# Moving a shared expert behind its 16 routed experts, and loading 8 experts' weights piece by piece among the next stage's rows, in a four-layer kernel

## The chip, the cores and the metric

The kernel runs on one core of a Trainium2 chip. The core has five engines with instruction queues of their own, each worked off in order: TensorE (PE, matrix products), VectorE (DVE), ScalarE (ACT), GpSimd (POOL) and SyncE (SP, which here issues most DMA transfers). The metric is the device time of one execution in microseconds (us), the median over several runs; the profile is one further execution.

## The reference

Four layers follow one another, each an "attention" (a token mixer) and an ffn, each behind a residual sum and a layer norm. x is (4, 1024, 128) in float32: 4096 tokens of 128 values.

```python
x = _layernorm(x + _L0_attn_ref(x, ...))   # cumulative sums over tokens
x = _layernorm(x + _L0_ffn_ref(x, ...))    # quantized linear layer
x = _layernorm(x + _L1_attn_ref(x, ...))   # complex diagonal recurrence
x = _layernorm(x + _L1_ffn_ref(x, ...))    # 16 experts, top 4, + shared expert
x = _layernorm(x + _L2_attn_ref(x, ...))   # causal softmax attention, 16 heads
x = _layernorm(x + _L2_ffn_ref(x, ...))    # 8 experts, top 2
x = _layernorm(x + _L3_attn_ref(x, ...))   # Toeplitz mixing, gated
x = _layernorm(x + _L3_ffn_ref(x, ...))    # experts, top 4, + shared expert
```

The change touches the ffn of layer 1 and the weights of the ffn of layer 2:

```python
# _L1_ffn_ref, E = 16 experts, F = 128
topk_idx, tw = _route(x, router_w, bias)             # 4 experts of each token
h = einsum('td,edf->etf', x, gate_w); u = einsum('td,edf->etf', x, up_w)
y = einsum('etf,efd->etd', silu(h) * u, down_w)
routed = einsum('etd,te->td', y, combine)
sh = silu(x @ sh_gate_w) * (x @ sh_up_w) @ sh_down_w # every token, 256 wide
return routed + sh

# _L2_ffn_ref, E = 8 experts, common weights plus low-rank parts of each expert
act = silu(x @ w_gate.T + d1[e]) * (x @ w_up.T + d3[e])
```

## The kernel before, in words

**Tokens.** x and its transpose stay in SBUF as 32 tiles of 128 tokens, in four quarters of 8 tiles. The first half ("a") is quarters 0 and 1, the second ("r") quarters 2 and 3. The halves run staggered: while one is in layer 1, the other is still in layer 0.

**Experts.** A routed ffn takes four steps. The router gives each token its experts and a place in each expert's list (`l1_route`, `positions`). `spread` (L1317) writes every token's row into the lists in DRAM (`l1ra`, `l1rr`): one indirect DMA (L1305) by POOL for each tile and choice, so 64 for a half with 4 experts a token. `small_experts` runs through the lists: 18 groups of 4 tiles, whose rows SP loads as `xg` (L1336); PE transposes them (`tp`), multiplies by gate and up (`gu`) and down; SP stores the result `yg` to `l1ya` or `l1yr` (L1762). A further part for longer lists stands in a branch. `collect` (L1385) fetches each token's results back by indirect DMA of POOL (`yt`, 5 buffers of four) and adds them to x with their weights (DVE, L1396).

**Shared expert.** `l1_shared` loads swg, swu and swd and runs four blocks of 4 tiles: two products `pg` and `pu` a half block (L157), hidden `hs` (DVE), the down product `py`, and the addition to x (DVE, L830). `l1_close` collects, norms a quarter, saves it (`xsave`, L840) and transposes it anew.

**Weights of layer 2.** `l2_weights` loads 1.5 MB (`in_l2_big`, in the profile `ld<-in_l_big`) and works out each expert's full weights on PE and ACT, since common weights and low-rank parts can be summed beforehand; 24 pieces go to DRAM (`wall_30`, L1450). `l2_wall` (L1467) loads them back into SBUF as `wall`, 8 transfers of 768 KB on SP (L1472), and `l2_experts` uses them.

**Order.** The stages are Python generators that emit instructions and yield planned microseconds. `chain` runs generators one after the other, `abreast` runs one beside another, `mix(main, side, pace, drain)` emits `side` whenever the planned time of `main` has run ahead, `when` yields until a condition holds. `queued` (L231) keeps what is emitted as side behind the latest main instruction of PE, ACT, DVE and POOL; SP's queue has no such tie. A list scheduler then settles each engine's order by dependencies and priority. Which step may begin is also set by memory: a pool's space is reused when its last reader has finished.

**Stages around the change** (`all`, L1882). First half: scatter to `l1ra`; then `l1_shared(a)` and `l1_experts(a)` as main, with `l0_ffn` and `l1_attn` of quarters 2 and 3 as side; then `l2_weights` and the rest of that side as main, with `l1_close(a)` as side. Second half: `l2_attn(0)` beside routing and scatter of r; then the 8 loads of `l2_wall`; then `l1_experts(r)` and `l1_shared(r)` as main, with `routed(a2)` (routing and scatter of the first half's rows for layer 2, list `l2ra`) as side; then `l2_experts(a2)` beside `l1_close(r)`.

Of the kernel before, what the change touches and what calls it, by code (L numbers as in the profile page):

```python
# [41 lines left out]
E2, F2, R2, K2 = 8, 512, 16, 2  # L42
# [32 lines left out]
class Kernel:  # L75
# [737 lines left out]
    def l1_shared(self, part):  # L813

        nc, x = self.nc, self.x
        with ExitStack() as ctx:
            cp = self.pool(ctx, "l1sc" + part.name)
            hp = self.pool(ctx, "l1sh" + part.name, 2)
            ps = self.pool(ctx, "l1sp" + part.name, 2, space=PSUM)
            swg = self.load(cp, self.ins["l1_swg"])  # L820
            swu = self.load(cp, self.ins["l1_swu"])
            swd = self.load(cp, self.ins["l1_swd"])
            for blk in range(part.t0 // 4, (part.t0 + part.nt) // 4):
                h = self.tile(hp, [P, 2, BLK], "hs")
                for c in range(2):
                    f = slice(c * P, (c + 1) * P)
                    self.glu(ps, hp, h[:, c, :], swg[:, f], swu[:, f], blk)
                py = self.down(ps, h, swd, 2)
                tl = slice(blk * 4, blk * 4 + 4)
                nc.vector.tensor_tensor(x[:, tl, :], py, x[:, tl, :], ALU.add)  # L830
                yield (5.5,)

    def l1_close(self, part, yp):

        nc, x = self.nc, self.x
        for q in range(part.q0, part.q0 + part.nq):
            yield from self.collect("l1", part, K1, yp, (q - part.q0) * QT, QT)
            self.norm(self.quarter(q))
            tl = slice(q * QT, (q + 1) * QT)
            nc.sync.dma_start(out=self.xsave[:, tl, :], in_=x[:, tl, :])  # L840
            yield (6.0,)
            for g in range(2):
                self.turned(self.side, q * QT + g * 4, tag="s")
                yield (1.5,)
# [619 lines left out]
            yield from self.positions(cp, "l2" + part.name, mask, w, part.nt, E2, K2)  # L1464
            yield (6.0,)

    def l2_wall(self, ctx):  # L1467
        cp = self.pool(ctx, "l2fw")
        wall = self.tile(cp, [P, E2 * 3 * F2], "wall")
        for e in range(E2):  # L1470
            c = slice(e * 3 * F2, (e + 1) * 3 * F2)
            self.nc.sync.dma_start(out=wall[:, c], in_=self.wall2[:, c])  # L1472
        return wall

    def l2_experts(self, part, wall):
# [406 lines left out]
    def all(self):  # L1882
        a, rest = self.first, self.rest
        b, c = rest
        r = self.both[1]
        a2, m2, n2 = self.by_rows
        with ExitStack() as ctx:
            lgp = self.pool(ctx, "l2lg")
            self.l2_lg = self.tile(lgp, [P, NT, E2], "lg")
            with ExitStack() as early:  # L1890

                self.l0_setup(early)
                self.l2_wr = self.load(lgp, self.ins["l2_wr"])
                self.run(self.l0_attn((0, 1)))
                self.l1_setup()
                self.l2_setup()
                self.zero_lists("l1")
                self.run(self.l0_ffn((0, 1)))
                self.run(self.l1_attn((0, 1)))

                self.run(self.l1_route(a))
                self.run(self.mix(self.l0_attn((2, 3), True), self.spread("l1", a, K1)))
                self.zero_lists("l2", "l3")
                with ExitStack() as c2:
                    wall = self.l1_wall(c2)
                    yp = self.pool(c2, "l1ya", 5, right=True)
                    side = self.chain(self.l0_ffn((2, 3), True), self.l1_attn((2, 3), True))
                    self.run(self.mix(self.chain(self.l1_shared(a), self.l1_experts(a, wall)), side, 2.0, False))
                    self.run(self.mix(self.abreast(self.l2_weights(), side), self.l1_close(a, yp)))
            with ExitStack() as c2:  # L1910
                wall = self.l1_wall(c2)
                self.run(self.mix(self.l2_attn(0), self.chain(self.l1_route(r), self.spread("l1", r, K1))))
                wall2 = self.l2_wall(c2)
                yp = self.pool(c2, "l1yr", 5, right=True)
                self.run(self.mix(self.chain(self.l1_experts(r, wall), self.l1_shared(r)), self.routed(a2)))
                self.run(self.mix(self.l2_experts(a2, wall2), self.l1_close(r, yp)))
            listed = lambda name: lambda: name in self.listed
            on = self.served(
                self.chain(self.rows_in(a2), self.onward(a, True)),
                (lambda: self.rows_done >= B + 2, self.routed(m2)),  # L1920
                (lambda: self.rows_done == 2 * B, self.routed(n2)),
            )
            self.run(self.mix(self.l2_attn(1), on, drain=False))
            with ExitStack() as c3:
                with ExitStack() as c2:
                    wall = self.l2_wall(c2)
                    self.press(on, listed("l2m"))
                    self.run(self.mix(self.l2_experts(m2, wall), on, drain=False))
                    self.press(on, lambda: {"l2n", "routed l3a"} <= self.listed)
                    sw, wall3 = self.l3_wall(c3, True)  # L1930
                    on = self.chain(on, self.rows_in(m2))
                    self.run(self.mix(self.l2_experts(n2, wall), on, drain=False))
                self.press(on, listed("l3a"))
                yp = self.pool(c3, "l3y", 8)

                on = self.chain(
                    on, self.collect("l2", n2, K2, yp, which=(0, 1, 4, 5)),
                    self.abreast(
                        self.chain(self.l3_attn(b), self.mark("mixed l3b"), self.l3_route(b)),
                        self.collect("l2", n2, K2, yp, which=(2, 3, 6, 7)),  # L1940
                    ),
                    self.abreast(
                        self.chain(self.spread("l3", b, K3), self.when(listed("made l3a")), self.last(a, yp)),
                        self.chain(self.l3_attn(c), self.mark("mixed l3c"), self.l3_route(c)),
                    ),
                    self.spread("l3", c, K3), self.when(listed("made l3b")), self.last(b, yp),
                )
                self.run(self.mix(self.chain(self.l3_shared(a, sw), self.l3_experts(a, wall3)), on, 0.75, False))
                hold = self.pool(c3, "l3hold", 2)
                for p in (b, c):  # L1950
                    self.press(on, listed("mixed l3" + p.name))
                    sh = self.tile(hold, [P, QT, D], "sh")
                    self.run(self.mix(self.l3_shared(p, sw, sh), on, 0.75, False))
                    self.press(on, listed("l3" + p.name))
                    self.run(self.mix(self.l3_experts(p, wall3), on, 0.75, p is c))
                    s = slice(p.t0, p.t0 + QT)
                    self.nc.vector.tensor_tensor(self.x[:, s, :], sh, self.x[:, s, :], ALU.add)
                self.run(self.close(c, yp))
        bad = self.nc.values_load(self.flag[0:1, 0:1], min_val=0, max_val=1)
        with self.tc.If(bad > 0):  # L1960
            with ExitStack() as ctx:
                lgp = self.pool(ctx, "l2lg2")
                self.l2_lg = self.tile(lgp, [P, NT, E2], "lg")
                self.l2_wr = self.load(lgp, self.ins["l2_wr"])
                self.l2_attn_general()
                for p in self.by_rows:
                    self.run(self.routed(p))
                    with ExitStack() as c2:
                        self.run(self.l2_experts(p, self.l2_wall(c2)))
                    self.run(self.rows_in(p))  # L1970
                for p in self.parts:
                    self.run(self.onward(p))
                    with ExitStack() as c2:
                        sw, wall = self.l3_wall(c2)
                        self.run(self.l3_shared(p, sw), self.l3_experts(p, wall))
                        self.run(self.last(p, self.pool(c2, "l3y" + p.name, 5)))
# [165 lines left out]
```

## Time and profile before

| what | value |
|---|---|
| times of 3 runs | 2420.16, 2432.44, 2435.95 us |
| median | 2432.44 us |
| the profiled execution: its time / its span | 2430.2 / 2428.4 us |
| mean granted PE clock of it | 0.821 |
| busy share of the span: PE, DVE, ACT, POOL | 66%, 52%, 33%, 32% |
| bytes moved by DMA | 187.11 MB, mean 77 GB/s |

How to read the profile: times are microseconds from the start of the span, unless marked ns. A timeline row gives the start, the busy time of a group of like instructions, the engine, the line in the kernel, the operation, output<-inputs by the kernel's names, the count, and in brackets how long the engine had been idle before and what ended that. "SPq" and the like are the engine's instruction queue, in which DMA is issued. "PEld" is the loading of weights into PE. A row of windows gives start and end of a stretch, its length, the busy time of each engine in it with the number of instructions, the granted PE clock (1.00 is full), the mean busy share of the 16 DMA engines, and what they moved. "<-issue" stands for idle time in which the engine waited for nothing that the profile shows.

### The profile page before, as it was taken

Reading aid. Unit: us, or ns where it says so; the run is one execution under the profiler, and the core shown is the slowest. Engines: PE = TensorE matmul, PEld = TensorE weight load, DVE = VectorE, ACT = ScalarE, POOL = GpSimd, SP = SyncE. Lnnn points to the kernel's source line nnn. Section 1 sums busy time; section 2 is a strip of 40 time slices with the busy share of each in tenths; the row PEclk is TensorE's granted clock in tenths of the full one; section 3 lists DMA queues with packets and bytes.
Section 4 is the critical chain, followed back from the end, with each engine's and each line's share of the span. In section 5 each row is a group of like instructions: output and inputs, shape, how many; then the busy total and the mean of one; then the engine's idle time right before and its main releaser. Section 6 shows DMA issues by size and latency. Waiting matters only on the chain. (4 is left out here: it accounts for less than half of the span.)

```text
span 2428.4 us, 27065 instructions
## 1 busy us (share of the span) xinstructions
PE 1597.9 (66%) x9017; PEld 952.6 (39%) x9017; DVE 1272.6 (52%) x3628; ACT 804.3 (33%) x1161; POOL 780.6 (32%) x701
## 2 busy tenths in 40 slices
PE   6535776866671675677969787887726798357160
PEld 2214433743330344544623232344414486145160
DVE  8767895655670564324535674573602265236233
ACT  5511372322330332212336554632201164223030
POOL 5531285145227002234132002002272200735724
PEclk9766788988785888888979998988867899679575
DMA  9930002334201014312130000031411131222232
GB/s 308 288 107 0 14 34 81 118 113 151 77 29 52 16 64 149 97 46 74 41 104 21 1 1 18 1 118 35 160 66 35 39 112 50 76 76 65 89 88 68
DMA packets 215531, 187.11 MB, mean 77 GB/s; under 512 B 16528, under 2 KB 194064, under 8 KB 214864
## 3 DMA queue, kind: packets, MB, share of 16 engines
q1 hardware_dynamic: 194672, 142.29, 18.5%
q0 software_dynamic: 20704, 42.86, 5.7%
q8 instruction: 84, 1.38, 0.2%
q14 instruction: 71, 0.58, 0.1%
HBM read 88.49 MB, written 96.60 MB: 76 GB/s over the span
## 5 line engine op out<-in xcount | busy, mean ns | idle before, releaser
L1059 ACT ACTIVATE pr<-sc 128x1024 f32<-128x1024 f32 x288 | 279.7, 1021 | 318.3 <-PE sc L157 189.2
L157 PE MATMUL gu<-ld,xgT 128*128 x640 | 173.4, 416 | 77.2 <-issue 39.2
L157 PE MATMUL sc<-qm,kT 32*128 32x512 f32 (+3 forms) x1536 | 200.3, 558 | 16.9 <-issue 9.7
L157 PE MATMUL s<-pr,va 128*32 128x512 f32 (+3 forms) x1536 | 173.9, 521 | 46.1 <-issue 26.3
L157 PEld LDWEIGHTS gu<-ld,xgT 128*128 128x128 f32 x640 | 125.5, 207 | 105.9 <-issue 50.0
L169 DVE COPY hT<-tp 128x512 f32<-128x512 f32 x118 | 81.0, 686 | 151.0 <-remote 75.8
L157 PE MATMUL gu<-wall,xgT 128*128 x304 | 156.2, 640 | 2.7 <-ACT xgT L167 2.0
L165 PE MATMUL tp<-ld,xg 128*128 128x128 f32 x396 | 67.2, 299 | 130.1 <-DMA xg<-l3rc 48.5
L165 PE MATMUL tp<-ld,hg 128*128 128x128 f32 x624 | 100.5, 282 | 77.0 <-issue 39.7
L1065 DVE TENSOR_TENSOR pr<-pr,ld 128x512 f32<-128x512 f32 (+1 forms) x160 | 92.3, 581 | 102.6 <-ACT pr L1059 96.5
L1744 DVE TENSOR_TENSOR hg<-sg,gu 128x256 f32<-128x256 f32 x160 | 65.7, 417 | 152.0 <-ACT sg L1743 104.2
L167 ACT COPY xgT<-tp 128x512 f32<-128x512 f32 x99 | 57.9, 586 | 243.5 <-PE tp L165 84.5
L157 PEld LDWEIGHTS sc<-qm,kT 32*128 32x128 f32 x1536 | 85.3, 196 | 117.2 <-issue 78.2
L165 PEld LDWEIGHTS tp<-ld,hg 128*128 128x128 f32 x624 | 79.3, 145 | 129.3 <-issue 74.1
L1743 ACT ACTIVATE sg<-gu 128x256 f32<-128x256 f32 x160 | 60.9, 385 | 166.4 <-PE gu L157 71.9
L1305 POOL DMA_INDIRECT l1ra<-x,posl1a x64 | 94.9, 1482 | 60.7 <-DVE posl1a L1280 41.5
L1502 ACT ACTIVATE sg<-gu 128x512 f32<-128x512 f32 x76 | 45.2, 597 | 206.5 <-PE gu L157 115.1
L1305 POOL DMA_INDIRECT yt<-l1yr,posl1r x64 | 60.7, 948 | 139.6 <-DVE x L1396 79.3
L165 PEld LDWEIGHTS tp<-ld,xg 128*128 128x128 f32 x396 | 50.3, 153 | 135.7 <-issue 83.7
L157 PEld LDWEIGHTS s<-pr,va 128*32 128x32 f32 x1536 | 38.6, 112 | 155.4 <-issue 108.0
L1305 POOL DMA_INDIRECT l1rr<-x,posl1r x64 | 62.5, 976 | 96.3 <-DVE posl1r L1280 77.1
L1305 POOL DMA_INDIRECT yt<-l1ya,posl1a x64 | 70.0, 1094 | 69.9 <-DVE x L1396 29.3
(444 smaller groups left out, 3505.8 us busy)
## 6 DMA issues: line engine op xcount, KB each, us to landing
wall<-wall SPq DMA_DIRECT2D x16, 768.0 KB
l3ra<-zero SPq DMA_DIRECT2D x1, 6144.0 KB
ld<-in_l_w SPq DMA_DIRECT2D x2, 3072.0 KB
wall<-we SPq DMA_DIRECT2D x24, 256.0 KB
ld<-in_l_w SPq DMA_DIRECT2D x1, 6144.0 KB
l1ra<-zero SPq DMA_DIRECT2D x1, 5120.0 KB
l1rr<-zero SPq DMA_DIRECT2D x1, 5120.0 KB
xg<-l3ra SPq DMA_DIRECT2D x20, 256.0 KB
```

The costliest lines, as they stand in the source:

```text
L157: return self.nc.tensor.matmul(out, lhsT, rhs, start=start, stop=stop)
L165: nc.tensor.transpose(pt[:, k * P : (k + 1) * P], s, self.ident)
L167: nc.scalar.copy(dst, pt[:, : n * P])
L169: nc.vector.tensor_copy(dst, pt[:, : n * P])
L1059: nc.scalar.activation(pr, sc[h], AF.Exp)
L1065: nc.vector.tensor_tensor(d, d, cst["tril"].unsqueeze(1).unsqueeze(1).to_broadcast([P, 2, n, P]), ALU.mult)
L1305: ins = self.nc.gpsimd.indirect_dma_start(**kw)
L1502: nc.scalar.activation(sg, gu[:, 0, :], AF.Silu)
L1743: nc.scalar.activation(sg, pg[:, :, 0, :], AF.Silu)
L1744: nc.vector.tensor_tensor(h[:, 2 * c : 2 * c + 2, :], sg, pg[:, :, 1, :], ALU.mult)
```

## The change

It has two parts. In the first half the shared expert of layer 1 goes from ahead of the 16 experts to behind them: it is then emitted in front of `l2_weights` and the rest of the side, and `l1_close(a)` runs beside all three. `l1_shared` notes when it is fully emitted, and `l1_close` holds each quarter's norm until then. In the second half `l2_wall` returns its 8 loads as a generator that yields 2.0 planned us after each, and they head the side of `l1_experts(r)`, with `routed(a2)` behind them, where before all 8 were emitted ahead of that stage. No instruction is added or removed by either part; the transfers and operations are the same in another order.

```diff
--- before.py
+++ after.py
@@ -829,12 +829,14 @@
                 tl = slice(blk * 4, blk * 4 + 4)
                 nc.vector.tensor_tensor(x[:, tl, :], py, x[:, tl, :], ALU.add)
                 yield (5.5,)
+        self.listed.add("shared l1" + part.name)
 
     def l1_close(self, part, yp):
 
         nc, x = self.nc, self.x
         for q in range(part.q0, part.q0 + part.nq):
             yield from self.collect("l1", part, K1, yp, (q - part.q0) * QT, QT)
+            yield from self.when(lambda: "shared l1" + part.name in self.listed)
             self.norm(self.quarter(q))
             tl = slice(q * QT, (q + 1) * QT)
             nc.sync.dma_start(out=self.xsave[:, tl, :], in_=x[:, tl, :])
@@ -1464,12 +1466,21 @@
             yield from self.positions(cp, "l2" + part.name, mask, w, part.nt, E2, K2)
             yield (6.0,)
 
-    def l2_wall(self, ctx):
+    def l2_wall(self, ctx, later=False):
+
         cp = self.pool(ctx, "l2fw")
         wall = self.tile(cp, [P, E2 * 3 * F2], "wall")
-        for e in range(E2):
-            c = slice(e * 3 * F2, (e + 1) * 3 * F2)
-            self.nc.sync.dma_start(out=wall[:, c], in_=self.wall2[:, c])
+
+        def load():
+            for e in range(E2):
+                c = slice(e * 3 * F2, (e + 1) * 3 * F2)
+                self.nc.sync.dma_start(out=wall[:, c], in_=self.wall2[:, c])
+                yield (2.0,)
+
+        if later:
+            return wall, load()
+        for _ in load():
+            pass
         return wall
 
     def l2_experts(self, part, wall):
@@ -1905,14 +1916,15 @@
                     wall = self.l1_wall(c2)
                     yp = self.pool(c2, "l1ya", 5, right=True)
                     side = self.chain(self.l0_ffn((2, 3), True), self.l1_attn((2, 3), True))
-                    self.run(self.mix(self.chain(self.l1_shared(a), self.l1_experts(a, wall)), side, 2.0, False))
-                    self.run(self.mix(self.abreast(self.l2_weights(), side), self.l1_close(a, yp)))
+                    self.run(self.mix(self.l1_experts(a, wall), side, 2.0, False))
+                    on = self.chain(self.l1_shared(a), self.abreast(self.l2_weights(), side))
+                    self.run(self.mix(on, self.l1_close(a, yp)))
             with ExitStack() as c2:
                 wall = self.l1_wall(c2)
                 self.run(self.mix(self.l2_attn(0), self.chain(self.l1_route(r), self.spread("l1", r, K1))))
-                wall2 = self.l2_wall(c2)
+                wall2, loads = self.l2_wall(c2, True)
                 yp = self.pool(c2, "l1yr", 5, right=True)
-                self.run(self.mix(self.chain(self.l1_experts(r, wall), self.l1_shared(r)), self.routed(a2)))
+                self.run(self.mix(self.chain(self.l1_experts(r, wall), self.l1_shared(r)), self.chain(loads, self.routed(a2))))
                 self.run(self.mix(self.l2_experts(a2, wall2), self.l1_close(r, yp)))
             listed = lambda name: lambda: name in self.listed
             on = self.served(
```

In the order that the scheduler gives, SP issues xg, xg, xg, two pieces, xg, two pieces, xg, a piece, a store of y, a piece, a store, xg, a piece, a store, a piece, and then xg and stores alone. In the first half SP issues swg, swu and swd, in_l_big and the weight stores behind the last y store of the experts; DVE has the last part of quarter 3's quantize, then the four shared blocks, then the first additions of `collect`.

## The prediction

> **What bounds the kernel now.** I read the busy totals first, then the timeline around the two places that the change touches, then windows by stage.
>
> No engine bounds the whole: TensorE (PE) is busiest, at 66%.
>
> ```profile
> PE 1597.9 (66%) x9017; PEld 952.6 (39%) x9017; DVE 1272.6 (52%) x3628; ACT 804.3 (33%) x1161; POOL 780.6 (32%) x701
> ```
>
> So I price each stage by itself. First place: the layer-1 ffn of the first half, from the last scatter to the last xsave (us from the span's start).
>
> ```profile
> 395.29 0.96 POOL L1305 DMA_INDIRECT l1ra<-x,posl1a  x1 [0.31 <-issue]
> 399.70 2.07 PE L157 MATMUL pg<-xT,ld 128*128 128x512 f32 x2 [11.87 <-DMA ld<-in_l_swg]
> 432.49 1.04 PE L165 MATMUL tp<-ld,xg 128*128 128x128 f32 x8
> 513.70 1.02 POOL L1305 DMA_INDIRECT yt<-l1ya,posl1a  x1 [21.98 <-DMA l1ya<-yg]
> 518.92 2.04 PE L157 MATMUL s<-ld,ld 128*128 128x512 f32 x2 [9.25 <-DMA ld<-in_l_big]
> 557.06 2.19 DVE L1396 SCALAR_TENSOR_TENSOR x<-yt,wkl1a,x 128x128 f32<-128x128 f32 x8
> 559.25 0.94 POOL L1305 DMA_INDIRECT yt<-l1ya,posl1a  x1 [17.10 <-DVE x L1396]
> 638.97 0.32 SPq L840 DMA_DIRECT2D xsave<-x  x1
> ```
>
> The shared expert holds PE from 399.70 to the experts at 432.49 (32.8 us); 81.2 us later the first row is gathered. From there POOL and the attention of quarters 2 and 3 share the time: 20 gathers fill the buffers, and the rest wait until DVE comes to its adds at 557.06.
>
> ```profile
> core 0: us, PE busy (x) PEld busy (x) DVE busy (x) ACT busy (x) POOL busy (x), PEclk, DMA share, GB/s
> 557.00:641.00 84.00, 41.38 (x152) 22.23 (x151) 47.02 (x182) 18.75 (x37) 47.36 (x44) 0.76 0.43 141
> 1033.00:1058.00 25.00, 13.61 (x36) 6.38 (x36) 3.31 (x5) 2.39 (x4) 18.98 (x20) 0.70 0.24 62
> 1058.00:1073.00 15.00, 14.01 (x64) 9.91 (x64) 4.90 (x8) 2.39 (x4) 0.00 (x0) 0.87 0.08 22
> 732.00:772.00 40.00, 8.61 (x20) 2.39 (x20) 2.05 (x6) 0.00 (x0) 30.38 (x32) 0.50 0.13 52
> ```
>
> In 557 to 641 no engine is full. The three rows below it say why: while POOL issues indirect DMAs the others thin out. In 1033 to 1058 shared blocks of the second half run beside 20 gathers, and PE works 13.61 of 25 us; right after, without gathers, 14.01 of 15. In 732 to 772, beside 32 scatters, PE is down to 8.61 of 40.
>
> Second place: layer-1 experts of the second half, with 8 loads of 768 KB (L1472) in front.
>
> ```profile
> 900.00:922.00 22.00, 4.54 (x22) 3.83 (x23) 6.85 (x31) 0.00 (x0) 0.00 (x0) 0.61 0.86 322
> ```
>
> ```profile
> 901.69 4.17 SPq L1472 DMA_DIRECT2D wall<-wall  x8
> 906.22 27.45 SPq L1336 DMA_DIRECT2D xg<-l1rr  x7
> 921.65 1.97 PE L165 MATMUL tp<-ld,xg 128*128 128x128 f32 x8 [10.66 <-DMA xg<-l1rr]
> 950.55 0.96 POOL L1305 DMA_INDIRECT l2ra<-x,posl2a  x1 [160.17 <-DVE posl2a L1280]
> 987.42 3.39 PE L157 MATMUL gu<-ld,xgT 128*128 x8 [28.06 <-issue]
> 1033.12 0.98 POOL L1305 DMA_INDIRECT yt<-l1yr,posl1r  x1 [42.13 <-DMA l1yr<-yg]
> 1033.68 2.04 PE L157 MATMUL pg<-xT,ld 128*128 128x512 f32 x2 [4.30 <-DMA ld<-in_l_swg]
> 1069.68 3.84 SPq L1336 DMA_DIRECT2D xg<-l2ra  x3
> 1072.36 0.69 DVE L830 TENSOR_TENSOR x<-py,x 128x512 f32<-128x512 f32 x1 [1.92 <-PE py L157]
> ```
>
> The DMA engines are 0.86 busy at 322 GB/s and PE waits 10.66 us for the first rows, which queue behind 6 MB. PE stalls again (28.06 us) in the burst of scatters from 950.55.
>
> **Part 1, the shared expert behind the experts.** Step by step:
>
> Experts start. The last scatter ends at 396.25. A store needs some 2.5 us to be seen by a reader (the last expert store is issued about 511, its reader goes at 513.70) and an xg load 2.8 us to PE (1069.68 to PE at 1072.50). So PE starts at 396.25 + 2.5 + 2.8 ≈ 401.5, and not at 432.49: 31 us earlier. The 3 MB of weights are in: at 399.70 swg, queued behind them on SP, had landed.
>
> Experts. 81.2 us, and some 5 more: in the schedule both quantizes of quarters 2 and 3 lie beside them, where one lay beside the shared expert, and with a quantize PE was busy 15.76 of 20 us (470 to 490), without 19.53 (450 to 470). Bounds 0 and 10. First gather: 401.5 + 86 ≈ 487.5, 26 earlier.
>
> Shared expert. SP issues swg, swu and swd behind the last y stores, as for the second half, where PE then ran beside 20 gathers from 1033.68 to 1073.05: 39 us. DVE has leftovers of the quantize in its queue ahead of the first shared block: 4 more. Bounds: 22 (four blocks at the 5.5 us of the undisturbed two) and 45. So 487.5 + 43 = 530.5. Queued behind it are in_l_big, whose memory comes free with it, and on DVE the first adds, which POOL's later gathers need: these start about 531 instead of 557.
>
> Weights of layer 2 and attention. From the issue of in_l_big (512.03) to PE's use of it (518.92) is 7 us: 537.5. Then come a rest of the ffn of quarter 3 (14), and attention: quarter 2 took 31.5 (525.66 to 557.14, the thin stretch of 531 to 539 costing about half its length), quarter 3 took 49.1 (561.62 to 610.7, with about 22 lost): 28 each unstarved, 56. The 24 stores of the layer-2 weights move on SP behind this; their readers, the loads of 901, have time to spare. The 3 MB load of the second half's layer-1 weights falls behind 23 of these stores and is due only at 921.
>
> Starvation. The 44 later gathers (44 × 1.26 = 55 us by the scatters' pace) run beside this attention. Before they cost it about 22 us (of 25 in 579 to 586 and 588 to 606, where DVE did one small operation per 2 us). I take 15, because more of them fall beside matmul work than beside small DVE operations; bounds 5 and 35.
>
> Tail. Norm of quarter 1 needs the last gathers: 24 adds at 0.29, the last gather and the norm, 17. End: 537.5 + 14 + 56 + 15 + 17 = 639.5 against 638.97: +0.5, between −27 and +20 with the bounds. What the 31 us gave is spent on a shared expert that is dearer beside gathers (43 + 7 for a load that it now holds back, against 33).
>
> The wait put into l1_close adds no semaphore by itself: norm reads the x that the shared adds write. It holds quarter 0's norm on DVE and behind it the first xsave; 12 weight stores queue on SP behind that xsave, none urgent.
>
> A rule of the Trainium skill speaks for more: "SBUF — State Buffer", section "Who interferes with whom", has PE and ACT never wait for another engine's SBUF access, and DVE contend with GpSimd only in certain modes. By it four shared blocks beside gathers would cost 22 us, not 39, and the whole about 2410 us. The rows of 1033 and of 732 disagree: there PE issues one matmul per 1.4 us, as below. The measurement decides; these sentences enter no sum.
>
> ```profile
> 752.22 0.37 PE L157 MATMUL s<-pr,va 128*32 128x128 f32 x1 [2.00 <-issue]
> ```
>
> **Part 2, eight loads behind the first groups.** On SP three xg loads now go first, then the pieces, among xg and y stores. Removed: 8 issues in front (4.17 us) and the queue in the DMA engines. PE's first work moves from 921.65 to about 912.5, held by DVE's copy in l2_attn's last step, which ends at 909.06, and a landing of 2.8: −9. Given back: the sixth to ninth xg now stand on SP behind y stores (which wait for their group) and pieces, where before they had 9 to 10 us of lead. A piece takes 768 KB / 322 GB/s = 2.4 us of all DMA engines; two or three in front of an xg that is due cost some 5. Bounds 0 and 12. Routing is emitted 16 planned us later, so the burst starts about 956; its 38 us stall stays inside the experts' stage (18 groups × 3.6 = 65 us of work), so moving it is worth 0. If it slid past the last y stores it would delay the gathers by some 6. Sum: −4, bounds −9 and +3. l2's experts need the pieces only at 1072.
>
> **Sum.** 2430.2 + 0.5 − 4 ≈ 2427. The profiled execution (span 2428.4, 1.8 outside it) is 2 us under the median of 2432.44, so I leave it.
>
> **Rivals.** (a) The shared expert is not starved. For it: before, it ran in 32.8 us beside a quantize, and its last two blocks of the second half took 5.5 each. Against: the row of 1033. Then part 1 gives its −27: 2430.2 − 27 − 4 ≈ 2399. (b) Slower: the later gathers, freed early, form one long burst beside the attention and stop it, as in 732 to 772 where PE kept 22%. Of 55 us, 43 or more are then lost (78%), 28 over my 15, and with the shared expert at its upper 45 and a second wait of POOL for adds behind quarter 3's work (17.10 before) some 40 in all: 2427 + 40 ≈ 2467. It decides from about 39 of the 55 us lost. Against: before, the same 44 gathers cost 22, because buffers fill and POOL waits for DVE, five at a time. (c) The pieces give back all of part 2, each xg being late by one piece: 4 to 9 us more, 2431 to 2436.
>
> **How the numbers follow.** 1% is 24 us, about what a measurement of this kernel can tell from no change. Forecast 0.48, (a) 0.2, (b) 0.2, (c) 0.12. Forecast and (c) lie within 1%, save some 0.02 at the slow end of their bounds and 0.01 at the fast end; of (a), 0.18 passes −24; of (b), all. That makes faster 0.19, within 0.59, slower 0.22. The range goes from (a)'s 2399 to 2459, where the lower part of (b) is in; the forecast's own bounds are 2430.2 − 36 and 2430.2 + 23.
>
> **What would show it.** First tp<-ld,xg of the first half near 401 (late if the rows land late); first l1ya gather near 487; shared pg to its last L830 add 39 to 45 us (22: rival a); first s<-ld,ld near 537; last xsave near 640 (over 665: rival b). In the second half PE's first tp near 912, the first l1yr gather near 1029. Wrong altogether if a later stage, untouched by the diff, changes its length by more than a few us.

## The result, and the profile after

The changed kernel takes 2433.09 us (median of 12 runs, 2427.39 to 2442.53), the kernel before 2430.57 us in 12 runs beside it: a ratio of 1.0025, 95% interval 1.0005 to 1.0046. Measured again later beside another set of runs it was 1.0012 (0.9994 to 1.003). So the change loses some 3 to 6 us or nothing, where the prediction's sum gave a gain of 3 us.

The profiled execution of the changed kernel has a span of 2427.1 us and a granted clock of 0.822. Its busy totals hardly move (first line of the page):

```profile
PE 1606.2 (66%) x9017; PEld 960.5 (40%) x9017; DVE 1273.1 (52%) x3628; ACT 803.8 (33%) x1161; POOL 783.1 (32%) x701
```

The timeline of the first half follows. Before the change's first difference this execution already runs 4.0 us later than the one before (the last scatter ends at 400.2 instead of 396.2), so 4 are to be taken off each time when it is held against the prediction.

```profile
399.26 0.96 POOL L1307 DMA_INDIRECT l1ra<-x,posl1a  x1 [0.30 <-issue]
407.18 1.97 PE L165 MATMUL tp<-ld,xg 128*128 128x128 f32 x8 [16.40 <-DMA xg<-l1ra]
488.52 2.04 PE L157 MATMUL pg<-xT,ld 128*128 128x512 f32 x2 [5.71 <-DVEq L1365]
490.77 2.00 POOL L1307 DMA_INDIRECT yt<-l1ya,posl1a  x1 [0.15 <-issue]
533.64 0.69 DVE L830 TENSOR_TENSOR x<-py,x 128x512 f32<-128x512 f32 x1 [1.92 <-PE py L157]
540.18 2.08 PE L157 MATMUL s<-ld,ld 128*128 128x512 f32 x2 [6.57 <-DMA ld<-in_l_big]
557.17 0.60 PE L165 MATMUL s<-ld,x 128*128 128x128 f32 x4
635.99 2.14 DVE L212 TENSOR_SCALAR x<-x,mv,rstd 128x128 f32<-128x128 f32 x8
654.16 0.33 SPq L842 DMA_DIRECT2D xsave<-x  x1
```

The experts start 25 us earlier and their results are fetched 23 us earlier; the shared expert takes 45.8 us (488.5 to 534.3) where it took 31.4; the layer-2 weights start 21 us later; and the last xsave, the end of the stage, comes at 654.2 instead of 639.0. At 557.17 the attention of quarter 2 begins with its transposes, and the row of 635.99 ends that of quarter 3 with its normalization.

The same for the second half:

```profile
920.55 2.86 SPq L1338 DMA_DIRECT2D xg<-l1rr  x3
923.58 0.84 SPq L1477 DMA_DIRECT2D wall<-wall  x2
931.62 1.95 PE L165 MATMUL tp<-ld,xg 128*128 128x128 f32 x8
961.36 1.09 PE L165 MATMUL tp<-ld,xg 128*128 128x128 f32 x4 [3.70 <-DMA xg<-l1rr]
982.16 0.96 POOL L1307 DMA_INDIRECT l2ra<-x,posl2a  x1 [172.32 <-DVE posl2a L1282]
1050.51 0.98 POOL L1307 DMA_INDIRECT yt<-l1yr,posl1r  x1 [28.19 <-DMA l1yr<-yg]
```

Three xg loads now go first and PE has its rows without a wait (931.62 has no idle time in front, 921.65 had 10.66); later an xg behind pieces makes PE wait 3.70. From the last scatter of l1rr to the first gather of l1yr it is 240.7 us against 242.7 before.

### The profile page after: what moved, and what is told of

Read it like the earlier page. It is cut to its first block, busy times and chain, and to the rows that moved or that the text cites. A ratio compares the mean times of both kernels' runs of the same rounds, so it can differ in the third digit from the quotient of the medians.

```text
span 2427.1 us, 27062 instructions
## 1 busy us (share of the span) xinstructions
PE 1606.2 (66%) x9017; PEld 960.5 (40%) x9017; DVE 1273.1 (52%) x3628; ACT 803.8 (33%) x1161; POOL 783.1 (32%) x701
## 5 line engine op out<-in xcount | busy, mean ns | idle before, releaser
L157 PE MATMUL gu<-ld,xgT 128*128 x640 | 179.7, 428 | 94.4 <-issue 38.2
L157 PE MATMUL s<-pr,va 128*32 128x512 f32 (+3 forms) x1536 | 174.1, 523 | 44.3 <-issue 24.4
L1515 DVE TENSOR_TENSOR hg<-sg,gu 128x512 f32<-128x512 f32 x76 | 51.6, 681 | 89.9 <-ACT sg L1513 46.7
```

The lines of the kernel that those rows point to most:

```text
L157: return self.nc.tensor.matmul(out, lhsT, rhs, start=start, stop=stop)
L1515: nc.vector.tensor_tensor(h, sg, gu[:, 1, :], ALU.mult)
```

## The experiments

Runs that were measured together share a chip and the runs of the kernel before; a ratio is always to that kernel on the same chip, with its 95% interval in brackets. On most chips that kernel took 2418 to 2432 us. One group (after_few, before_few, pace15, beside_rl) fell on a chip where it took 2076 us; its runs are compared with each other and with what the first 640 us show, and the four kernels were run again on slower chips (names ending in _c).

### Each part alone, a delay, and second profiles

p1_alone undoes the second part, p2_alone the first:

```diff
# p1_alone, against the changed kernel
-wall2, loads = self.l2_wall(c2, True)
+wall2 = self.l2_wall(c2)
-self.run(self.mix(self.chain(self.l1_experts(r, wall), self.l1_shared(r)), self.chain(loads, self.routed(a2))))
+self.run(self.mix(self.chain(self.l1_experts(r, wall), self.l1_shared(r)), self.routed(a2)))
# p2_alone, against the changed kernel (the first line stands in l1_close)
-yield from self.when(lambda: "shared l1" + part.name in self.listed)
-self.run(self.mix(self.l1_experts(a, wall), side, 2.0, False))
-on = self.chain(self.l1_shared(a), self.abreast(self.l2_weights(), side))
-self.run(self.mix(on, self.l1_close(a, yp)))
+self.run(self.mix(self.chain(self.l1_shared(a), self.l1_experts(a, wall)), side, 2.0, False))
+self.run(self.mix(self.abreast(self.l2_weights(), side), self.l1_close(a, yp)))
# delay_20, against the kernel before, between norm and xsave in l1_close
+if q == 1:
+    for _ in range(16):
+        nc.vector.tensor_tensor(x[:, tl, :], x[:, tl, :], x[:, tl, :], ALU.max)
```

p1_alone: 

> The first part alone (shared expert behind the 16 experts; the 8 loads in front of the second half's experts, as before). Theory: the whole loss sits in the first part, after the layer-2 weights begin: attention of quarter 2 starts 28 us later than before, loses time to the gathers and to additions on DVE, and the last xsave comes at 648 to 655 (before 638.97); the end loses 5 to 12 us, so 2436 to 2443. Rival: the first part is even and the pieces cost the time: last xsave within 3 us of 639, end 2428 to 2432.

Measured: 1.0028 (1.0002 to 1.0055), last xsave at 649.3 with the scatters' end where it was (396.0). The loss sits in the first part, and both numbers lie where they were expected.

p2_alone: 

> The second part alone (8 loads piece by piece; shared expert ahead of the experts as before). Theory: first tp<-ld,xg of the second half some 9 us earlier, the first l1yr gather some 4 us earlier (1029), end 2424 to 2430. Rival: the pieces in front of the sixth to ninth xg and the later scatter burst cost more than the earlier start gives: first l1yr gather at 1036 or later, end 2434 to 2440.

Measured: 0.9962 (0.9937 to 0.9987). First experts' rows at PE at 911.4 (921.7 before), first l1yr gather at 1029.2 (1033.1). The second part gains, and its stage moves as forecast; the whole gains some 9 us (3 to 15), more than was expected.

delay_20: 

> The kernel before with 16 more maxima of x with itself (x is unchanged) on DVE between quarter 1's norm and its xsave: a delay of 16 x 1.2 = 19 us at 637, where nothing else runs. Theory: the later stages absorb part of a delay that early, so the end loses only 6 to 12 us (2437 to 2443). Rival: nothing absorbs it, the end loses all 19 (2450).

Measured: 1.0068 (1.0039 to 1.0097), 9 to 24 us. The last xsave comes at 663.2, of which 20 us are the delay. A loss of the full 20 lies inside the interval, so nothing shows that later stages absorb a delay, and the theory has no support.

after_again: 

> The changed kernel once more, for a second profile. Expected: from the last scatter of the first half to the last xsave within 3 us of the first profile's 254 us; how far the second half's burst stalls and the end differ from it shows what one profile's late differences are worth (up to 10 us).

Measured: from the last scatter's end to the last xsave 260.4 us instead of 253.9, twice the 3 us that were allowed for, so the stage itself varies. The span is 2447.8, and the 20 us to the first profile arise behind the first l2ya gather (1208.3 us from there to the end, against 1187.0).

before_again: 

> The kernel before once more, for a second profile. In the first profiles the changed kernel stood 19 us behind at the first l2ya gather (1221 before) but level at the end; from there to the end before took 1207 us and five other kernels with the same instructions there 1187 to 1208 (mean 1199). Theory: that late part varies from run to run by some 10 us whatever the change, and before's first profile had a long one: now 1190 to 1204, and the first l2ya gather within 3 us of 1221. Rival: the early part is what varies, the gather comes at 1226 or later.

Measured: the part behind the gather takes 1192.2 us, as the theory had it, but the gather comes at 1226.1, where the rival had it (1.8 us of the difference were there at the last scatter). So both parts vary, the late one more. Over 14 profiles of ten kernels on chips of the slower kind the late part takes 1187 to 1208 us (the few kernels below, which carry other values, are left out: 1179.4 and 1193.0); three profiles of before have a mean of 1199, three of the changed kernel 1196. One profile's late differences are worth 10 us, and that the first two profiles ended level was an accident of this kind.

### Where the shared expert stands

hold keeps the gathers back with a POOL addition that reads the shared expert's last result; last puts the shared expert behind the attention; beside lets the attention run beside it:

```diff
-on = self.chain(self.l1_shared(a), self.abreast(self.l2_weights(), side))
# hold
+self.run(self.l1_shared(a))
+held = self.tile(yp, [P, P], "yt")
+self.nc.gpsimd.tensor_tensor(held, self.x[:, t9, :], self.x[:, t9, :], ALU.add)   # t9: last tile of a
+on = self.abreast(self.l2_weights(), side)
# last
+on = self.chain(self.abreast(self.l2_weights(), side), self.l1_shared(a))
# beside
+on = self.abreast(self.chain(self.l1_shared(a), self.l2_weights()), side)
```

hold: 

> The changed kernel, with the gathers of the first half held back until the shared expert's last addition (one small POOL addition that reads it stands in POOL's queue ahead of them). Theory: the shared expert is starved by the 20 gathers beside it, so without them it takes 22 to 27 us from first pg to last L830 addition (43 to 48 beside gathers), PE's first use of in_l_big comes some 20 us earlier, at 512 to 520, and the stage ends like before's, last xsave 636 to 645. Rival: the shared expert is slow there for another reason (leftovers of the quantize on DVE, its weights' loads): it still takes 38 us or more, and the last xsave, with gathers 40 us later, comes after 660.

Measured: 1.0017 (0.9991 to 1.0042). The shared expert takes 28.4 us instead of 45.8 (from 489.36 to the end of this addition), so the gathers beside it do cost it 17 us:

```profile
517.03 0.69 DVE L830 TENSOR_TENSOR x<-py,x 128x512 f32<-128x512 f32 x1 [1.92 <-PE py L157]
```

PE uses in_l_big at 523.5, with a start 4.6 us late: the same place as before the change. But the last xsave still comes at 654.1. Half of the theory fell: with gathers and weights starting where they did before, the stage ends 10 us later all the same. The trace shows where: from the first use of in_l_big to the attention's first transposes it is 28.1 us here and 3.5 before, since the rest of quarter 3's layer-0 ffn, now beside the gathers, stands in between; attention and tail are shorter by less than that (78.1 and 24.4 us against 88.2 and 28.3).

last: 

> The changed kernel, with the shared expert behind the layer-2 weights and the attention of quarters 2 and 3 instead of ahead of them. Theory: what the first part loses is that weights and attention wait for the starved shared expert; without this wait they start at 490 to 500 (540 in the changed kernel), the shared blocks find room at the end, the last xsave comes at 612 to 632 and the whole takes 2405 to 2420. Rival: the gathers' starvation only moves to the attention and the norms wait for the late shared expert: last xsave 639 or later, 2425 or more.

Measured: 1.0017 (1.0000 to 1.0034). The weights start at 488.4, 48 us earlier than in the changed kernel (counted from the last scatter), but the last xsave comes at 650.4: the theory fell. The attention ends at 597.6, the shared expert runs from 598.0 to 622.3 (24.3 us, without gathers), and the norms wait for it. Whether the shared expert stands in front of the attention or behind it, one waits for the other.

beside: 

> The changed kernel, with the attention of quarters 2 and 3 beside the shared expert and the layer-2 weights instead of behind the shared expert. Theory: the attention of quarter 2 starts some 15 us earlier, as in the changed kernel PE stands idle in the starved shared blocks; the weights stay where they are (their load needs the shared expert's memory); last xsave 638 to 648, whole 2418 to 2428. Rival: idle PE beside gathers is of no use to others, and the last xsave stays at 650 to 656.

Measured: 0.9943 (0.9923 to 0.9963), last xsave at 635.7. Only here do two pieces of work overlap that stood behind each other. The shared expert takes longer (53.2 us) and in_l_big is used at 543.2, but the attention starts 24 us earlier (counted from the last scatter), and the first part's loss is gone: 240.6 us from the last scatter to the last xsave, where the kernel before takes 238 to 243.

### What the gathers cost, and quarter 3's ffn

The few kernels fetch one row instead of four for each token of the first half (the additions read it four times), which leaves out 48 of 64 gathers and keeps every other instruction of the stage; x then has other values than the reference. pace15 emits the side at pace 1.5 beside the 16 experts.

```diff
# after_few, before_few: in collect, few = (lay + part.name == "l1a")
-    self.x[:, part.order[t], :], yt[:, i, :], wk[:, t, i : i + 1], ...
+    self.x[:, part.order[t], :], yt[:, 0 if few else i, :], wk[:, t, i : i + 1], ...
-for i in range(k):
+for i in range(1 if few else k):
     self.indirect(out=yt[:, i, :], ...)
# pace15, against the changed kernel
-self.run(self.mix(self.l1_experts(a, wall), side, 2.0, False))
+self.run(self.mix(self.l1_experts(a, wall), side, 1.5, False))
```

after_few: 

> The changed kernel with one gather per tile instead of four in the first half's collect (16 instead of 64; the additions all read the one that is fetched, so this stage's sum is not the reference's). It measures by itself what the gathers cost the work beside them. Theory: without most of them the shared expert takes 24 to 31 us instead of 46 to 47, the attention of quarters 2 and 3 some 56 to 66 us instead of 81 (first transposes of quarter 2 to the end of quarter 3's normalization), and the last xsave comes at 605 to 622. Rival: the attention is slow because of the layer-2 weights and the additions on PE and DVE, not the gathers: still 75 us or more, last xsave after 632.

before_few: 

> The same in the kernel before (16 gathers instead of 64, the same part left out). Theory: the attention takes 56 to 66 us instead of 85 to 88, as much less as in the changed kernel, so what the gathers cost it is the same in both, 20 to 30 us; last xsave 600 to 618. Rival: before, the gathers cost it much less than after (my prediction's 15 against 22 the other way round): 75 us or more.

after_few_c: 

> One gather per tile in the changed kernel's first half. On the slow chip: theory, shared expert 24 to 31 us (46 with all gathers), attention of quarters 2 and 3 56 to 70 us (81), last xsave 605 to 628; rival, attention 75 us or more and last xsave after 632. On the fast one: the same as the first time (34 and 69 us, 627.2), and against after_c it tells what 48 gathers cost there: theory under 10 us, rival 20 or more.

before_few_c: 

> One gather per tile in the kernel before, again (the first time fell on the chip where before takes 2076 us). Theory: the attention of quarters 2 and 3 takes 58 to 64 us here as well (60.5 there; 69 in the changed kernel with few gathers on both chips), since quarter 0's additions and norm stand behind it on DVE and not in its midst; last xsave 600 to 610. Rival: it takes 66 us or more, and the two kernels' attention differs by nothing but the gathers; last xsave 612 or later.

Measured, from quarter 2's first transposes to the end of quarter 3's normalization: 69.0 and 69.1 us in the changed kernel (two chips; after_few's theory had 56 to 66), 60.4 and 60.4 in the kernel before (two chips). With all gathers it is 76.3 to 82.4 in four profiles that hold the first part of the change, 84 to 88 in four of the kernel before or of p2_alone. So the gathers that were left out cost the attention 24 to 28 us before and 7 to 13 after (mean 11), not the same in both as before_few expected; and without them the attention is 9 us longer in the changed kernel. One reason for the smaller cost is in the traces: 45 gathers lie beside the attention before, 32 after, and 8 in either few kernel.

The shared expert took 34.3 and 34.6 us with few gathers, more than expected but well under 45.8. The last xsave came at 627.2 and 632.8 in the changed kernel, 5 us behind what the theories had, and at 603.6 and 608.4 in the kernel before. So even with most gathers gone the changed order ends 23 us later, counted from the last scatter, and no theory had that. On the slower chips these 23 are +8 up to the first use of in_l_big, +14 for the rest of quarter 3's ffn, +9 for the attention and −7 for the tail. Here are the windows, first the changed kernel, then before, each over its attention with all gathers:

```profile
557.00:639.00 82.00, 53.46 (x215) 31.99 (x214) 54.08 (x189) 21.55 (x45) 36.29 (x32) 0.84 0.39 138
```

```profile
522.00:611.00 89.00, 55.87 (x219) 31.13 (x218) 47.40 (x155) 21.20 (x47) 50.15 (x46) 0.86 0.41 136
```

and the same with few gathers, after_few_c and before_few_c:

```profile
550.00:619.00 69.00, 51.60 (x213) 31.06 (x210) 52.41 (x183) 21.03 (x44) 12.09 (x8) 0.91 0.36 136
```

```profile
527.00:588.00 61.00, 51.85 (x219) 30.47 (x217) 46.39 (x156) 21.27 (x47) 8.68 (x8) 0.98 0.41 148
```

PE and ACT do nearly the same work in all four. DVE does 6 to 7 us more in the changed kernel, in 27 to 34 more instructions: mostly quarter 0's norm, which stands inside the attention in the changed kernel and behind it before. The additions of `collect` do not make this difference: 32 of them lie within the attention in each of the four, and not behind it as the expectation of before_few_c has it. But they lie elsewhere. Before the change they are all quarter 0's, 8 between the two quarters' attention and 24 in quarter 3's, and none between quarter 2's transposes and its norm; afterwards 24 of quarter 0's fall into quarter 2's attention and 8 of quarter 1's into quarter 3's.

The timelines show what that does. In the changed kernel (first fence) 16 of these additions stand between the two scans of quarter 2's attention, and the statistics of quarter 0's norm (bn) behind them, and PE waits 8.18 us for the attention's product `g`. Before (second fence) the two scans follow each other, and quarter 0's norm (615.11) comes behind quarter 3's (608.55).

```profile
567.93 4.27 DVE L1398 SCALAR_TENSOR_TENSOR x<-yt,wkl1a,x 128x128 f32<-128x128 f32 x16
572.12 2.28 DVE L653 TENSOR_TENSOR_SCAN g<-l1keep,b 128x1024 f32<-128x1024 f32 x1
574.32 0.46 DVE L192 BATCH_NORM_STATS2 bn<-x 128x6 f32<-128x128 f32 x2
...
578.61 1.17 DVE L671 TENSOR_TENSOR g<-g,pw 128x1024 f32<-128x1024 f32 x1
579.70 2.23 DVE L212 TENSOR_SCALAR x<-x,mv,rstd 128x128 f32<-128x128 f32 x8
579.92 3.75 PE L157 MATMUL s<-l1c,g 128*128 128x128 f32 x16 [8.18 <-DVE g L671]
```

```profile
533.61 4.47 DVE L653 TENSOR_TENSOR_SCAN g<-l1keep,b 128x1024 f32<-128x1024 f32 x2
...
540.07 1.22 DVE L671 TENSOR_TENSOR g<-g,pw 128x1024 f32<-128x1024 f32 x1
...
608.55 2.14 DVE L212 TENSOR_SCALAR x<-x,mv,rstd 128x128 f32<-128x128 f32 x8
615.11 2.13 DVE L212 TENSOR_SCALAR x<-x,mv,rstd 128x128 f32<-128x128 f32 x8
```

From the first scan's start to the end of the last `g` it is 14.1 us (565.73 to 579.78) against 7.7 (533.61 to 541.29), and the 6.4 us more are nearly all the 16 additions (4.2) and the statistics (2.0) in between. With few gathers it is the same 14.1 and 7.6 (after_few_c, before_few_c). There quarter 2's attention takes 39.9 us instead of 27.5 and quarter 3's 29.2 instead of 32.9, and PE's waits for DVE within the attention add up to 16.5 us instead of 8.8, which is 7.7 of the 9. No run moves the additions or the norm alone, so the price of each by itself is not shown. The kernel last agrees: there the norm stands behind the attention, as many gathers lie beside it as in the changed kernel, and it takes 74.3 us; but some of the weights' work is out of its way as well.

pace15: 

> The changed kernel with the side work of the 16 experts at pace 1.5 instead of 2.0, so that as much of it is emitted beside the experts alone as before beside shared expert and experts; quarter 3's layer-0 ffn is then again emitted in front of the shared expert. Theory: a part of the first part's loss is this ffn, which the shorter main leaves for the stage behind; it returns beside the experts, which take 3 to 6 us longer; last xsave 640 to 648 (654 and 655), end 2420 to 2430. Rival: the attention is bound by the gathers' end whatever is left in front: last xsave 651 or later, end 2430 or more.

pace15_c: 

> Pace 1.5 in the first half on this chip. On the fast one: as in the first run, 2055 to 2062, and against after_c it tells what quarter 3's ffn in the late stage costs: theory 5 to 14 us, rival less than 3. On the slow one: theory, last xsave 640 to 648 (654 and 655 at pace 2.0), end 2420 to 2430; rival, last xsave 651 or later, end 2430 or more.

after_c: 

> The changed kernel beside it. On the fast chip: theory, where gathers do not starve the others the moved shared expert costs some 25 us beside them instead of 46, so the first part turns into a gain, last xsave 8 to 20 us before before_c's, and the whole is faster by 10 to 30 us (2046 to 2066); rival, the loss does not depend on starvation: 2076 or more. On the slow chip: 0 to 12 us slower, as the first time.

Measured: pace15 0.9911 (0.9886 to 0.9935) on the chip where before takes 2076 us; the changed kernel itself was not timed there, so what it would win there stays open. Side by side on a slower chip after_c took 1.0012 (0.9994 to 1.003) and pace15_c 0.9993 (0.9971 to 1.0014). The last xsave of pace15_c, 643.5, lies where it was expected, but that of after_c beside it came at 644.3, so the 6 to 15 us that the theory wanted (640 to 648 against 654 and 655) are not there. The ffn did move ahead of the shared expert, and the attention ends 9 us earlier (619.1 against 628.3). But the last gather comes at 638.1 against 637.3, and the close waits for it: the additions that free the gathers' buffers stand on DVE behind the attention. The stage has two chains of nearly equal length, the attention and the gathers, and when one is shortened the other sets the end.

before_c: 

> The kernel before, for its profile on this chip. If the kernel takes 2076 us here: theory, the stages up to the last xsave (639) are within 20 us of the first chip's, the shared expert of the second half takes 25 us or less instead of 39, and PE is not held up by 28 us in the scatters of l2ra; rival: all stages are faster by the same 15%. If it takes 2431: last xsave 638 to 640, and a third sample of the part behind the first l2ya gather (1187 to 1208 so far).

Measured: it takes 2420 us here, so the second case holds: last xsave 636.0, 2 us earlier than expected, late part 1196.3, within the span of the others.

### The pieces of weights

beside_rl is beside with the routing in front of the loads:

```diff
-self.chain(loads, self.routed(a2))
+self.chain(self.routed(a2), loads)
```

beside_rl: 

> The version with the attention beside the shared expert, and in the second half the routing emitted ahead of the 8 loads. Theory: what the second part gives back lies in pieces and stores of y in front of the sixth to ninth xg; with fewer pieces there the first l1yr gather comes at 1022 to 1028 (1030 with the loads first, 1033 before), end 2410 to 2418. Rival: the stall in the scatters sets that stage, and an earlier burst gives nothing: first gather 1029 or later, end 2416 to 2424.

beside_rl_c: 

> Attention beside the shared expert, and routing ahead of the 8 loads, on this chip. Theory: last xsave 633 to 640 as in the version with the loads first (635.7), first l1yr gather 1022 to 1028 as fewer pieces stand ahead of the sixth to ninth xg (1030), whole 0.986 to 0.993 of before. Rival: the stall in the scatters sets that stage, first gather 1029 or later, ratio 0.994 or more.

Measured: 0.986 (0.9829 to 0.9891) on the chip where before takes 2076 us, 0.9958 (0.9934 to 0.9982) on one where it takes 2420. On the latter the last xsave (637.7) and the first l1yr gather (1025.2, 5 us earlier than in beside) come where they were expected, but the ratio does not: 0.986 to 0.993 was the theory, and 0.994 or more the rival. The scatters begin at 942.64 (961.2 in beside). From its timeline:

```profile
942.64 0.96 POOL L1307 DMA_INDIRECT l2ra<-x,posl2a  x1 [151.60 <-DVE posl2a L1282]
```

The earlier burst and the freer queue were changed together, so how the 5 us divide between them stays open. The three versions that beat both kernels, p2_alone, beside and beside_rl_c, cannot be told apart in time (their intervals overlap).

## Why the prediction was wrong, point by point

**Up to 540 the sum held.** Less the late start of 4.0 us, the profile after gives: experts' first rows at PE 403.2 (forecast 401.5), first gather 486.8 (487.5), end of the shared expert 530.3 (530.5), first use of in_l_big 536.2 (537.5). That the shared expert would take 43 to 46 us beside gathers, and not 22, was right, and hold shows the reason: 28.4 us without them. Rival (a) is out.

**The step that failed is the attention term.** The first part in four stretches, in us from the last scatter's end; the measured values are means of four profiles each (after, after_again, after_c, p1_alone; before, before_again, before_c, p2_alone):

| stretch | forecast | measured after | measured before |
|---|---|---|---|
| last scatter to first use of in_l_big | 141.3 | 140.2 | 122.8 |
| from there to quarter 2's transposes (rest of quarter 3's ffn) | 14 | 17.6 | 3.5 |
| attention of quarters 2 and 3, with starvation | 56 + 15 = 71 | 80.2 | 86.3 |
| from there to the last xsave (tail) | 17 | 16.0 | 28.5 |
| sum | 243.3 | 253.9 (248.0 to 260.4) | 241.0 (238.4 to 242.8) |

So part 1 was priced at +0.5 and lost 13, and the attention term makes most of the gap: it was to take 71 us and took 80, the ffn was 3 short, and the rest held. Within the 80 the few runs give 69 and some 11. Starvation came near its 15, in part by luck: the 11 us are for 24 gathers more beside the attention, and 32 in all lay there, not the 44 that the prediction counted. "28 each unstarved" was 13 short. Of these 13, 4 were a misreading of before itself: it takes 60, not 56, since the prediction's two windows leave out 7.7 us of the stretch from 522.46 to 610.69, and how much of each stall counted was a guess. The other 9 the change made: gathers that come earlier free quarter 0's additions and norm earlier, and DVE, which works its queue off in order, does 24 of the additions and the norm's statistics within quarter 2's attention. The prediction counted the earlier additions ("these start about 531 instead of 557") only as a gain. It did name DVE's queue, and did not ask who waits behind them: PE, 8.18 us at 579.92.

**Readings of the prediction that do not hold.** "PE issues one matmul per 1.4 us" is not what its rows say: they have 20 matmuls in 40 us and 36 in 25. The bounds of part 1, −27 and +20, are not the sum of its terms' own bounds, which would be about −36 and +27. Neither entered the sum.

**Part 2 was right in size, partly for another reason.** −9 at the first rows and −4 at the first gather were forecast; p2_alone shows −10.2 and −3.9. From the last l1rr scatter to the first l1yr gather, three profiles of before, p1_alone and delay_20 need 242.7 to 245.0 us, and the ten profiles on the slower chips with the pieces behind the first xg 234.1 to 241.0. What follows DVE's copy is not a landing of 2.8 us, as I had it: xg is issued at 900.4 in p2_alone, and PE itself is busy with the last products of the attention step until 911.4. The give-back was there (a 3.10 us wait for xg at 940.16 in p2_alone). The time of p2_alone fell by 9 us (3 to 15), for which its stage gives only 4.

**Rivals.** (b), attention stopped almost fully by the later gathers, did not come: they cost it some 11 us, not 43. (c) did not come either: p2_alone gains.

**From stage to end.** Stage by stage the change loses some 13 us at the last xsave (four profiles against four with the old first half) and wins 5 in the second half, so 8 are expected; by the times it is 6 and 3 (whose intervals reach to 11 and 7). The two parts alone, 6.8 lost and 9.2 won, would even add up to a gain of 2, though their intervals allow the loss. With a late part that varies from 1187 to 1208 us, the difference is not settled by these runs, and no experiment shows a place where it is given back.

## What to carry to other kernels

Work that is made ready earlier also gets earlier into an in-order queue: for each instruction that a faster step frees, ask what stands behind it on its engine. A block moved from ahead of a stage to behind it gains nothing when all that follows waits for it; here its loss went away only when the next work was put beside it (beside), so that the two overlapped, and even then the stage was no shorter than before. Where a term rests on an undisturbed duration that no row shows, measure it by a version that leaves the disturbance out, before trusting a sum that comes out at zero.

## What the runs showed of the hardware

One kernel, two chips. Here is the stretch of 32 scatters of l2ra for pace15 on the chip where the kernel before takes 2076 us, and for the same file on one where it takes 2418:

```profile
871.40:911.50 40.10, 35.88 (x220) 30.08 (x219) 18.56 (x43) 14.01 (x29) 30.64 (x32) 0.96 0.48 154
```

```profile
967.00:1007.50 40.50, 13.95 (x81) 12.01 (x79) 6.46 (x20) 3.87 (x8) 30.88 (x32) 0.73 0.24 83
```

The columns are those of the windows above: POOL issues the same 32 scatters in the same 40 us, and PE works 35.88 us beside them on the one chip and 13.95 on the other. The two profiles of this kernel run level for the first 490 us and differ by 349 us at the end (spans of 2067.8 and 2416.8). In the first burst (64 scatters of l1ra) PE is busy 35.05 us of the stretch from 340 to 397 on both, so not every burst tells the chips apart. The Trainium skill ("SBUF — State Buffer", section "Who interferes with whom") says that PE and ACT never wait for another engine's access to SBUF; for DVE it names instructions with two SBUF inputs beside certain modes, which the prediction left out. The first chip's 35.88 of 40.10 us agrees with it. On the second PE is idle for 26.6 us, and 16.7 of them end with ACT's copy of xgT; no row shows an SBUF access as what was waited for, so the page is not refuted, but it does not tell what to expect there. Since the file is the same, the starvation of the other engines during bursts of indirect DMA is not a property of the kernel alone. What makes the chips differ no run here shows. For a kernel like this it means that the same order can be worth different amounts on different chips: beside_rl wins 1.4% on the one and 0.4% on the other.
